# One decoder layer on one core: the self-attention regrouped into a score phase and a value phase

## The chip, the cores and the metric

The kernel runs on one core of one Trainium2 chip. The metric is device time in microseconds, the median of the runs shown; less is better. The core has a matrix engine (TensorE, in the profile PE, its weight loads PEld), VectorE (DVE), ScalarE (ACT), GpSimd (POOL) and SyncE (SP), and 16 DMA engines that move data between on-chip memory and HBM. In this kernel SP and POOL issue the DMAs. Matrix products go to eight PSUM banks of 128 x 512 float32 and are carried from there by ScalarE or VectorE.

## The reference

`x` is 4 batches of 512 rows of 512. Three blocks follow one another, each with a layer norm before it and a residual after it:

```python
x = x + attn(layernorm(x), Wq, bq, Wk, bk, Wv, bv, Wo, bo)   # 16 heads
x = x + xattn(layernorm(x), ctx, ctx, gamma)                 # 8 heads, cross attention
x = x + ffn(layernorm(x), w1, w3, w2)                        # ternary weights, silu gate

def attn(x, ...):                      # T=512 rows, 128 channels a head
    q = (x @ Wq + bq).reshape(B, T, 128, 16)   # and k, v
    q = transpose(q, (0, 3, 2, 1))             # channels x rows
    k = transpose(k, (0, 3, 1, 2))             # rows x channels
    v = transpose(v, (0, 3, 2, 1))             # channels x rows
    att = softmax(q @ k / sqrt(128))           # 128 x 128, a head
    return reshape(att @ v) @ Wo + bo
```

The attention is between channels, not between rows: a head's score matrix is 128 x 128, whatever the number of rows. The feed-forward's weights are quantized to -1, 0, 1 times a scale (the mean of the absolute values); its hidden width is 1365.

## The kernel before, in words

**What is multiplied.** Since scores are q'·k over the rows, the kernel never builds q and k. For each batch it takes the normalised rows X, forms the gram matrix G = X'X (512 x 512; `gram_upper`, L422, computes the blocks on and above the diagonal, `gram_rest`, L451, turns the others on TensorE), then y = G·Wk for a quarter of the heads (`keys_of`, L483; a quarter is four heads, 512 columns, index j) and the scores Wq'·y, four 128 x 128 blocks (`scores`, L503, with the softmax). On the other side u = X'·Wo-part (`values_out`, L468), m = Wv'·u (`values_of`, L493), and the result rows are the sum over heads of turned scores times m (`output`, L545, into four accumulators a batch that start as x plus the bias). `turned` (L540) transposes the scores on TensorE.

**Split products.** A plain float32 product is 16 matmuls, each done as two passes. A split product (`products`, L329) has its operands in three float32r parts, h, l and d (`Tri`, `tri_of`, L187: h on ScalarE, l and d on VectorE): per pair of output blocks 16 matmuls h and l into one bank each (L336, L337), a copy to memory by ScalarE (L343, a tile of `a_t`), 8 matmuls of d (L348), and one VectorE operation that joins them (`total`, L356). A split product is 48 matmuls.

**Batch 0** (L865 to L939) brings the raw weights of each quarter (`first_weights`, L234; the last row of a weight is folded in, L255, to take account of the bias row), makes their parts and keeps them in HBM for the other batches (`keep_weights`, L258, with DMAs issued by POOL; q is kept unsplit). While parts are being made, six of its twelve products are plain (`products_f32`, L363): u and y of quarter 0 and the m of all four quarters (`FIRST`, L213).

**Batches 1 to 3** (L977 to L1021) load the kept parts of o, k and v and the kept q (`weights`, L302, DMAs issued by SP into the 18 buffers of `a_w`; in batch 1 the missing d parts are made, L322, and kept) and run for every quarter u, y, m and the scores; turned scores and outputs come one quarter later. Beside them, in small steps taken at each `tick` of a product, run the quantization of the feed-forward's weights (`quantize`, 73 steps over three batches) and the cross attention of the batch before (`cross`, L680: scores in two matmuls, maximum and scaling on VectorE, exponential on ScalarE, transposes, and a product with 64 columns). The cross attention of batch 3 runs in the feed-forward.

**The feed-forward** (L1055 to L1130) loads the quantized weights as three resident tiles t1, t3 and t2 and runs h1, h3 (L1084) and y (L1119) for each batch.

**Order.** The code is written for a planner that orders each engine's instructions: it takes the earliest in the program that it reckons to be ready, so an instruction that is not ready is passed by later ones, and the order is then fixed for the run. Semaphores keep it right. `issue_after` and `gate_of` (L218: a constant that is computed from a given tile, so that what uses it can't be placed before that tile is there) hold work back. Each engine and each issuing queue goes through its list in order, and a waiting instruction holds what is behind it.

**Memory.** On-chip memory is a stack from the left and one from the right (`side="right"`), and it is nearly full. A pool that is closed makes room for later ones, whose tiles wait until the old tiles in that place are done with (`reuse_waits="tile"`: for each tile by itself).

## Time and profile before

| | |
|---|---|
| time, median of 3 runs | 1152.13 us (1150.59 to 1153.99) |
| span of the profiled execution | 1150.0 us |
| median of the runs less that span | 2.1 us |
| busy: TensorE, weight loads, VectorE, ScalarE, GpSimd | 99%, 75%, 71%, 46%, 26% of the span |
| granted TensorE clock | 0.999 |
| moved by DMA | 270.68 MB |
| batch 0 (first matmul of its gram to the next gram) | 6.90 to 190.25 us |
| next grams, of batches 1, 2, 3, start at | 190.25, 409.28, 624.51 us |
| first feed-forward matmul | 852.45 us |

The profile's page gives busy time by engine, a picture of the span in slices, the DMA queues, the chain of work that ended last, and the costliest groups of instructions. A time on its own, as "0.44 us", is a duration; "at 104 us" is counted from the span's start. A matmul is pipelined: its duration (some 0.39 us for 512 float32r columns) is longer than the distance to the next, so a busy share near 100% alone does not say how much time a set of matmuls takes. The distance between the starts of neighbours does.

### The profile page before, as it was taken

What the parts mean: (1) busy time and instruction counts of PE and PEld (TensorE: products, weight loads), DVE (VectorE), ACT (ScalarE), POOL (GpSimd) and SP (SyncE); (2) the same over time, 40 slices, a digit from 0 to 9 for tenths busy, and PEclk for the clock granted to TensorE, in tenths of its full rate; (3) what the DMA queues carried; (4) which work ended last, traced back from release to release, by engine and by line L of the source; (5) the groups of instructions that cost most, each with busy time, mean ns of one, the idle gap of its engine ahead of it and who ended that gap; (6) DMA issues with size and microseconds to landing.
All of it is one profiled execution on the core that took longest, in us unless ns stands there. A gap on an engine that the chain in (4) does not pass through costs nothing.

```text
span 1150.0 us, 16662 instructions
## 1 busy us (share of the span) xinstructions
PE 1140.7 (99%) x5310; PEld 858.6 (75%) x5310; DVE 818.7 (71%) x1818; ACT 523.5 (46%) x1071; POOL 295.9 (26%) x534
## 2 busy tenths in 40 slices
PE   9999999999999999999999999999999999999998
PEld 5486585787778767877776787777778877777886
DVE  6857766978788965969696769788857856536242
ACT  4534334354535442644354445445355768534020
POOL 3435433433133232213221422122113212000000
PEclk9999999999999999999999999999999999999999
DMA  9999996998889769988986798799791422122100
GB/s 332 306 344 337 345 314 225 324 319 280 281 281 308 261 201 325 312 272 276 321 291 215 256 334 271 254 330 325 268 304 40 122 79 65 48 73 72 64 1 37
DMA packets 146177, 270.68 MB, mean 235 GB/s; under 512 B 18276, under 2 KB 49300, under 8 KB 146090
## 3 DMA queue, kind: packets, MB, share of 16 engines
q1 hardware_dynamic: 112218, 164.93, 43.4%
q0 software_dynamic: 33872, 104.70, 26.8%
q8 instruction: 42, 0.69, 0.2%
q14 instruction: 45, 0.37, 0.1%
HBM read 206.62 MB, written 62.93 MB: 234 GB/s over the span
## 4 chain that ended last, share of the span: by engine, by line
PE 96%; DMA 2%; DVE 1%; issue 1%; ACT 0%; POOL 0%; SPq 0%; DVEq 0%; POOLq 0%; ACTq 0%
PE h L1084 13%; PE y L1119 7%; PE xo L770 5%; PE xp L126 5%; PE po L548 5%; PE pm L370 5%; PE sc L509 5%; PE pg L430 3%; PE xs L727 3%; PE xs L726 2%; PE pu_2h L336 1%; PE pu_1d L348 1%; PE py_3h L336 1%; PE py_3h L337 1%; PE pu_2h L337 1%; PE py_2h L337 1%
## 5 line engine op out<-in xcount | busy, mean ns | idle before, releaser
L1084 PE MATMUL h<-fxh,t 128*128 128x512 f32 (+1 forms) x352 | 139.6, 397 | 0.0
L1084 PE MATMUL h<-fxl,t 128*128 128x512 f32 (+1 forms) x352 | 137.4, 390 | 0.0
L737 ACT ACTIVATE p<-xs,xnmax 128x512 f32<-128x512 f32 x128 | 87.2, 689 | 84.8 <-PE xp L126 68.2
L731 DVE TENSOR_REDUCE xnmax<-xs 128x1 f32<-128x512 f32 x128 | 83.5, 684 | 19.3 <-PE xs L727 19.3
L1084 PEld LDWEIGHTS h<-fxh,t 128*128 128x128 f32 (+1 forms) x352 | 65.0, 185 | 15.4 <-issue 1.1
L1084 PEld LDWEIGHTS h<-fxl,t 128*128 128x128 f32 (+1 forms) x352 | 65.0, 185 | 14.7 <-issue 0.2
L1119 PE MATMUL y<-t,gh 128*128 128x512 f32 (+1 forms) x176 | 69.3, 394 | 0.0
L1119 PE MATMUL y<-t,gl 128*128 128x512 f32 (+1 forms) x176 | 68.8, 391 | 0.0
L129 ACT COPY pt<-xp 128x512 f32<-128x512 f32 x96 | 54.1, 595 | 31.0 <-PE xp L126 31.0
L126 PE MATMUL xp<-ident,p 128*128 128x128 f32 x512 | 66.5, 273 | 0.0
L126 PEld LDWEIGHTS xp<-ident,p 128*128 128x128 f32 x512 | 59.3, 140 | 9.4 <-issue 2.4
L770 PE MATMUL xo<-pt,vals 128*64 128x512 f32 x256 | 61.5, 599 | 0.0
L1097 DVE SCALAR_TENSOR_TENSOR gf<-h,scales_w,sl 128x512 f32<-128x512 f32 (+1 forms) x44 | 32.9, 747 | 39.8 <-PE h L1084 36.4
L749 DVE TENSOR_SCALAR p<-p,xrden 128x512 f32<-128x512 f32 x128 | 56.7, 486 | 2.9
L548 PE MATMUL po<-m,eT 128*128 128x512 f32 x128 | 57.6, 593 | 0.0
L1093 ACT ACTIVATE sl<-h,scales_w 128x512 f32<-128x512 f32 (+1 forms) x44 | 30.1, 688 | 58.7 <-PE h L1084 58.5
L689 POOL DMA_DIRECT2D xd<-x_a x64 | 33.8, 532 | 88.6 <-DVE qs L710 64.5
L370 PE MATMUL pm<-u,v_raw 128*128 128x512 f32 x128 | 55.6, 592 | 0.0
L727 PE MATMUL xs<-kl,qs 128*128 128x512 f32 x128 | 50.1, 391 | 0.5 <-DVE kl L714 0.5
L138 POOL CAST gh<-gf 128x512 fp32r<-128x512 f32 (+1 forms) x24 | 15.8, 660 | 134.9 <-DVE gf L1097 119.7
L726 PE MATMUL xs<-kh,qs 128*128 128x512 f32 x128 | 50.1, 392 | 0.0
L139 DVE TENSOR_TENSOR gl<-gf,gh 128x512 fp32r<-128x512 f32 (+1 forms) x44 | 30.4, 690 | 26.3 <-POOL gh L138 19.3
(313 smaller groups left out, 2897.6 us busy)
## 6 DMA issues: line engine op xcount, KB each, us to landing
oh<-kept_oh SPq DMA_DIRECT2D x48, 256.0 KB, 5.9
ol<-kept_ol SPq DMA_DIRECT2D x48, 256.0 KB, 6.2
kh<-kept_kh SPq DMA_DIRECT2D x48, 256.0 KB, 5.2
kl<-kept_kl SPq DMA_DIRECT2D x48, 256.0 KB, 5.9
vh<-kept_vh SPq DMA_DIRECT2D x48, 256.0 KB, 6.6
vl<-kept_vl SPq DMA_DIRECT2D x48, 256.0 KB, 6.9
q<-kept_q SPq DMA_DIRECT2D x48, 256.0 KB, 6.6
od<-kept_od SPq DMA_DIRECT2D x44, 256.0 KB, 6.8
```

Of the source, the lines that this page charges most:

```text
L126: nc.tensor.transpose(pt[:, ts(k, P)], src[:, ts(k, P)], ident)
L370: nc.tensor.matmul(p, lhsT=lhs(k)[:, ts(i, P)], rhs=rhs(k), start=(k == 0), stop=(k == 3))
L509: nc.tensor.matmul(sc[:, ts(g, DH)], lhsT=w[k][:, ts(g, DH)], rhs=ys[k][:, ts(g, DH)], start=(k == 0), stop=(k == KC - 1),)
L548: nc.tensor.matmul(po, lhsT=eT[:, g, :], rhs=ms[g], start=True, stop=True)
L726: nc.tensor.matmul(sc, lhsT=q[:, ts(m, P)], rhs=kh, start=True, stop=False)
L727: nc.tensor.matmul(sc, lhsT=q[:, ts(m, P)], rhs=kl, start=False, stop=True)
L731: nc.vector.reduce_max(nmax[:, i : i + 1], scs[i], axis=AX.X)
L737: nc.scalar.activation(p, scs[i], AF.Exp, bias=nmax[:, i : i + 1], scale=xscale, accum_out=den[:, i : i + 1],)
L749: nc.vector.tensor_scalar(ps[i], ps[i], rden[:, i : i + 1], None, ALU.mult)
L770: nc.tensor.matmul(po[half, :], lhsT=vals[c][:, l, half], rhs=pt[j][:, l, :], start=(l == 0), stop=(l == NC - 1),)
L1084: nc.tensor.matmul(ph[:r, :], lhsT=t[:, block(i, k)], rhs=fxT[j][:, k, :], start=(k == 0 and j == 0), stop=(k == KC - 1 and j == 1),)
L1119: nc.tensor.matmul(py, lhsT=g[i][j][:r, ts(c, P)], rhs=t2[:r, i, :], start=(i == 0 and j == 0), stop=(i == NHC - 1 and j == 1),)
```

## The change

The attention is regrouped into two phases.

**Score phase.** Sixteen steps, quarter by quarter and within each over the four batches. A step runs y (`keys_of`), then the scores of the step before, then turns the scores of two steps before. The k weights of a quarter are brought raw, folded and split once and stay on chip for its four steps (`keys_halves`, `keys_thirds`); q is folded once a quarter (`queries_folded`) after y of batch 1, by the newest gate. All four batches' split gram matrices stay on chip (those of batch 0 in the buffers of x's parts); rows are normalised and their grams formed ahead of, and during, the first steps. `y` tiles and gram matrices share eight buffers. Normalised rows go to HBM (`kept_x`), so do the turned scores (`kept_e`), written over the scores' own tile. From step 4 on, beside the products, the parts of o and v are made and kept (`kept_weights`, 32 pieces, DMAs in and out issued by POOL, five buffers for the parts).

**Value phase.** Batch by batch and quarter by quarter u, m and the output, with the rows and turned scores loaded back; all of these products are split. Weights come through 21 buffers. Quantization is spread over all four batches; cross attention of the batch before runs over the 48 ticks of a batch (42 in the last). Cross attention's second scaling moves from VectorE to ScalarE. The plain products and the parts they needed (`products_f32`, `FIRST`, `first_weights`, `keep_weights`) are gone.

The diff, cut to its core:

```diff
-    x3p, xnp, g3p, u3p = apool("a_x3", 12), apool("a_xn", 4), apool("a_g3", 1), apool("a_u3", 12)
-    yp, tp = apool("a_y", 5), apool("a_t", 3)
-    ep, mp, accp = apool("a_e", 1), apool("a_m", 4), apool("a_acc", 4)
+    x3p, tp, ep = apool("a_x3", 12), apool("a_t", 3), apool("a_e", 3)
...
+    def fold(k, t, last, gate):
+        less = gate[2 if k == KC - 1 else 1]
+        nc.vector.scalar_tensor_tensor(t, last, less, t, ALU.mult, ALU.add)
+
+    def halves_of_weight(h, l, t, gate):
+        nc.scalar.mul(h, t, gate[0])
+        nc.vector.scalar_tensor_tensor(l, h.bitcast(F32), -S, t, ALU.mult, ALU.add)
+
+    def third_of_weight(tri):
+        nc.vector.tensor_tensor(tri.d, tri.l.bitcast(F32), tri.h.bitcast(F32), ALU.subtract)
+
+    def keys_halves(j, k, raw, gate):
+        last, chunks = raw
+        fold(k, chunks[k], last, gate)
+        h, l = (kp.tile([P, GW], F32R, tag="k", name=f"k{p}_{j}_{k}") for p in "hl")
+        halves_of_weight(h, l, chunks[k], gate)
+        keys[j][k] = Tri(h, l, None)
...
+        coming = []
+        for item in itertools.chain(items(), [None]):
+            if item is not None:
+                coming.append((item[:3], bring(*item[:3])))
+                if len(coming) < 2:
+                    continue
+            (n, j, k), t = coming.pop(0)
+            gate = gates[0]
+            if n == "v":
+                fold(k, t, sources[j][0], gate)
+            tri = Tri(
+                *(pool.tile([P, GW], F32R, tag="made", bufs=5, name=f"{n}{p}_{j}_{k}") for p in "hld")
+            )
+            halves_of_weight(tri.h, tri.l, t, gate)
+            third_of_weight(tri)
+            for p, part in zip("hld", (tri.h, tri.l, tri.d)):
+                nc.gpsimd.dma_start(kept[n, j, p][ts(k, P), :], part.bitcast(F32))
+            yield
...
     def turned(b, j, e):
-        eT = ep.tile([P, NG, DH], F32, tag="eT", name=f"eT_{b}_{j}")
-        transpose_blocks(eT, e, f"pe_{b}_{j}", True)
-        return eT
+        transpose_blocks(e.rearrange("p (g t) -> p g t", g=NG), e, f"pe_{b}_{j}", True)
+        nc.gpsimd.dma_start(kept_e[b, j], e)
+
+    def turned_kept(b, j):
+        e = ep.tile([P, GW], F32, tag="e", name=f"eT_{b}_{j}")
+        nc.gpsimd.dma_start(e, kept_e[b, j])
+        return e
...
-            for i in range(2):
-                nc.vector.tensor_scalar(ps[i], ps[i], rden[:, i : i + 1], None, ALU.mult)
+            nc.vector.tensor_scalar(ps[0], ps[0], rden[:, 0:1], None, ALU.mult)
+            nc.scalar.mul(ps[1], ps[1], rden[:, 1:2])
...
+    kp, yp = apool("a_k", 20, phase_a), apool("a_y", 8, phase_a)
+    g3p = {b: apool(f"a_g3_{b}", 1, phase_a) for b in (3, 2, 1)}
+    qp = apool("a_q", 4, phase_a, side="right")
+    krp = apool("a_kr", 4, phase_a, side="right")
+    xpool = ExitStack()
+    xnp = apool("a_xn", 2 * NG, xpool, side="right")
...
+    grams[0] = gram_upper(0, xs)
+    raw_k = raw_all("k", 0, krp)
+    xs = rows_given(1)
+    for k in range(KC):
+        keys_halves(0, k, raw_k, gates[0])
+    normed(1, xs, False)
+    raw_q = raw_all("q", 0, qp)
+
+    def first_rest():
+        g3[0] = gram_rest(0, grams[0])
+
+    grams[1] = gram_upper(1, xs, first_rest)
+    keys_thirds(0)
...
+    for n, (j, b) in enumerate(STEPS):
+        if n == 4:
+            xpool.close()
+            ovp = apool("a_ov", 1, phase_a, side="right")
+            side = Side(kept_weights(ovp), KEPT_STEPS, 6 * (len(STEPS) - n) - 4)
+        if n < 2:
+            xs = rows_given(n + 2)
+            normed(n + 2, xs, False)
+        ys[n] = keys_of(b, j, g3[b], keys[j], side.tick)
+        gates[0] = gate_of(ys[n][3])
+        if n < 3:
+            g3[n + 1] = gram_rest(n + 1, grams[n + 1])
+        if n < 2:
+            grams[n + 2] = gram_upper(n + 2, xs)
+        if b == 1:
+            queries_folded(j)
+        if n > 0:
+            scored(n - 1)
+        if b == 0 and n > 0:
+            raw_q = raw_all("q", j, qp)
+        if b == 0 and j + 1 < HG:
+            raw_k = raw_all("k", j + 1, krp)
+        if b in (1, 2) and j + 1 < HG:
+            for k in CHUNKS[2 * (b - 1) : 2 * b]:
+                keys_halves(j + 1, k, raw_k, gates[0])
+        if b == B - 1 and j + 1 < HG:
+            keys_thirds(j + 1)
+        if n > 1:
+            turn(n - 2)
+        if n == len(STEPS) - 3:
+            xs = rows_kept(0, krp, "raw_k")
+        if n == len(STEPS) - 2:
             x3 = parts_of(0, xs)
...
+    side.rest()
+    scored(len(STEPS) - 1)
+    phase_a.close()
...
+    u3p, mp = apool("a_u3", 12), apool("a_m", 4)
+    accp, xnp, bop = apool("a_acc", 8), apool("a_xn_kept", 4), apool("a_bo", 1)
...
-        for n, k in (("a_w", 18), ("a_stage", 3))
+        for n, k in (("a_w", 21), ("a_stage", 3))
...
+    PRODUCT = 6
+    TICKS = 2 * HG * PRODUCT
+    quant = Side(quantize(), QUANTIZE_STEPS, B * TICKS - PRODUCT)
...
+    for b in range(B):
         for j in range(HG):
             u3 = values_out(b, j, x3, weights("o", b, j, wp), tick)
-            if j > 0:
-                waiting[2] = turned(*waiting[:3])
-            ys = keys_of(b, j, g3, weights("k", b, j, wp), tick)
-            if j > 0:
+            if b == 0 and j == 0:
+                turn(len(STEPS) - 2)
+                turn(len(STEPS) - 1)
+            if waiting:
                 output(*waiting)
...
+                if b > 0:
+                    side = Side(
+                        itertools.chain(row_norms(b - 1, accs), cross(b - 1, *cpool)),
+                        NORM_STEPS + CROSS_STEPS,
+                        TICKS if b + 1 < B else TICKS - PRODUCT,
+                    )
+                accs = accumulators(b)
...
+            eT = turned_kept(b, j)
             ms = values_of(b, j, weights("v", b, j, wp), u3, tick)
-            e = scores(b, j, weights("q", b, j, wp), ys)
...
+            waiting = [b, j, eT, ms, accs]
```

## The prediction

> **What bounds the kernel now.** I read the share of the span by engine, the chain, TensorE's own waits, then busy time by stretches. The first three lines are from the page, the waits follow.
>
> ```profile
> span 1150.0 us, 16662 instructions
> PE 1140.7 (99%) x5310; PEld 858.6 (75%) x5310; DVE 818.7 (71%) x1818; ACT 523.5 (46%) x1071; POOL 295.9 (26%) x534
> ...
> PE 96%; DMA 2%; DVE 1%; issue 1%; ACT 0%; POOL 0%; SPq 0%; DVEq 0%; POOLq 0%; ACTq 0%
> ```
>
> ```profile
> PE py_0d L348 <- DMA kd<-kept_kd: 1.0, 2, 0.6
> PE pm_0d L348 <- DVE vd L322: 0.9, 1, 0.9
> PE pu_1d L348 <- DMA od<-kept_od: 0.7, 1, 0.7
> ```
>
> TensorE runs from 6.90 us to the end with almost no holes, 96% of the chain is its work, and its waits on weights come to 2.6 us. So the change is worth what it takes off TensorE, less every new hole. Durations of single matmuls overlap; what counts is the spacing in the chain:
>
> ```profile
> 15.80 13.74 PE pu L370 x32
> ...
> 86.95 13.73 PE pm L370 x32
> ...
> 107.90 1.81 PE pu_2d L348 x8
> 113.34 1.81 PE pu_2d L348 x8
> 118.78 1.82 PE py_2d L348 x8
> ...
> 623.51 1.00 PE xo L770 x2
> 624.51 1.91 PE pg L430 x4
> 626.43 3.58 PE xo L770 x14
> ```
>
> A plain f32 product (32 passes at L370) takes 13.74 us. A split product repeats its half every 5.44 us (107.90, 113.34, 118.78), so it takes 10.88 us. The last three lines show that the planner reorders TensorE: the gram matrix of the next batch stands later in the program than the cross attention it interrupts.
>
> By stretches (columns: length, busy time of PE, PEld, DVE, ACT, POOL with counts, clock, DMA share, GB/s):
>
> ```profile
> 104.00:147.00 43.00, 43.00 (x176) 29.60 (x174) 30.96 (x65) 16.34 (x33) 20.61 (x39) 1.00 1.01 357
> 216.00:262.00 46.00, 44.43 (x216) 36.59 (x215) 39.67 (x94) 22.62 (x47) 14.34 (x26) 1.00 1.01 337
> 350.00:404.00 54.00, 54.00 (x280) 42.51 (x279) 50.04 (x125) 28.71 (x64) 12.79 (x22) 1.00 0.84 278
> 420.00:460.00 40.00, 38.96 (x183) 31.03 (x182) 28.11 (x65) 14.20 (x26) 12.77 (x23) 1.00 0.88 289
> 625.00:680.00 55.00, 55.00 (x250) 41.01 (x249) 34.73 (x81) 18.28 (x35) 17.04 (x31) 1.00 0.81 263
> ```
>
> VectorE at 93% (350:404) costs TensorE nothing. The DMA engines are full at 337 to 357 GB/s; the stretch at 337 lost 1.57 us, the one at 289 lost 1.04, the one at 263 nothing.
>
> **Part 1, TensorE's work.** Six products of batch 0 are plain today (u and y of quarter 0, the four of m); afterwards all 48 are split: 6 x (13.74 - 10.88) = 17.2 us less. All else on TensorE keeps its count: 4 grams, 16 scores (3.57 each), 16 turns, 16 outputs (3.43 each), cross attention, feed-forward. **-17.2.**
>
> By mean duration nothing would be gained (48 x 392 ns = 18.8 us against 32 x 592 ns = 18.9). The Trainium skill (Perfetto Trace Analysis, Identifying the Most-Contended Engine) rejects matmul busy time as a measure and takes the weight loads' share instead. That share is 75% here and would leave a quarter of the engine to absorb every new hole of the parts below, for 1132 us; the spacing above shows no such room, so the sum goes by spacing.
>
> **Part 2, waits that go.** The k loads and the making of vd and od in batch 1 disappear: **-2.6**, the three lines of waits.
>
> **Part 3, the start.** TensorE's first gram ends at 15.8 and was followed by a plain product on weights already there. Now the gram of batch 1 follows and needs that batch's rows normalised. On SP's queue they come behind the k weights: issue of x ends at 2.6, k_last takes 0.43, four k_raw 4.59, the rows 1.82, so the rows are issued from 7.6 to 9.4 and, at 4.7 us to landing, are there from 12.3 to 14.1. VectorE then needs the last statistics (0.68 + 0.17), the root (0.30, ScalarE), the reciprocal (0.15), the first tile (0.54 + 0.06): 16.0, a hole of 0.2. But four folds and four low halves of k (8 x 0.69 = 5.5 us) stand ahead of it; VectorE is free of batch 0 at 10.7, so 1.6 of them fit before 12.3 and 3.9 do not: hole 4.1. Ends: 0 (rows first) and 5.7 (none fits). **+4.1**, by program order.
>
> **Part 4, steps 0 to 3.** VectorE carries three row norms (about 7 us each), four gram splits (8 x 0.69 = 5.5 each), totals, scores and the next k: some 82 us by sum, against 85 of TensorE. Besides, the gram matrices and the y tiles share 8 buffers: y of step 1 and 2 wait until a gram is split, which stands behind them in the program, and TensorE goes on only as far as its 8 banks reach. Ends: 0 (20 to 60 us ran with VectorE at 28.10 of 40.00 and no hole) and 5.5, one gram split exposed. **+1**, near the first row.
>
> **Part 5, the other score steps.** One takes 10.88 + 3.57 + 0.44 = 14.9 us. In four steps (59.6 us) VectorE has 16 totals 10.9, four scores 8.7 (0.69, 0.17, 0.18, 4 x 0.284), q folds 3.0, k 8.5, gates 1.8, and 11.3 kept pieces of o and v at 1.75 each, 19.7: 52.6, or 88%, under the 93% that cost nothing. The q fold is gated on y of batch 1, so that step's scores are ready only two totals, a gate and four folds later (1.4 + 0.45 + 3.0 = 4.8). Behind them on TensorE stand a turn and the next product, which the planner can take first, as with pg above: 0; unfilled, in steps 5, 9 and 13, 14.4. The kept pieces use five buffers for three parts each: a part is held for making (0.72 + 2 x 0.69), an issue on POOL (0.54) and a landing (4.0 to 7.1 by the store rows), 6.6 to 9.7 us, so a piece can follow every 4.0 to 5.8 us; one is wanted every 5.6: 0, other end 32 x 0.2 = 8. POOL issues four DMAs a piece, 2.2 of 5.6 us, and SP loses the k and q loads: 0. **0.**
>
> **Part 6, values of batch 0.** 4 x (2 x 10.88 + 3.43) = 100.8 us, with no cross attention beside it. Transfers, in tiles of 0.262 MB: weights 96, quantization 22 (73 steps over 186 ticks, 48 here), turned scores 4, accumulators and bias 5, rows 4, result 4: 135, or 35.3 MB, 350 GB/s. The 21 weight buffers lie on the gram tiles of batches 1 and 2, free by the last score step, so 12 or more tiles come ahead: 32.2 MB, 319 GB/s. The nearest row is 337 GB/s, losing 1.57 in 46: 3.4 in 101. Ends: 0 (357) and 13.8 (nothing comes ahead, at the 308 GB/s of the first 20 us: 114.6 us for 35.3 MB). **+3.4.**
>
> The Trainium skill (DMA: Bandwidth & Descriptors, Where 436 GB/s comes from) puts the HBM limit of a core at about 358 GB/s, which would make this part 0 and the sum 1142; two full stretches here differ by 20 GB/s, so the slower one stays in the sum.
>
> **Part 7, first quarters of batches 1 to 3.** There cross attention is only starting: some 44 tiles, 11.5 MB, 34.2 us at 337, against about 27.5 on TensorE; nine spare buffers cover 7.0. Nearest rows are today's first quarters (1.57, 1.04, 0): **+2.6** in all. Ends 0 and 3 x 6.7 = 20. VectorE over such a batch: 140 us by sum; measured busy in 404 to 625 is 171.3 where the same count gives 185, so 130 of 145: 0. If the last quarters run out of VectorE, 3 each. The scaling moved to ScalarE takes 64 x 0.486 = 31 us from VectorE: 0, ScalarE is half idle.
>
> **Part 8, into the feed-forward.** Its second weight tile (t3) now lies on the turned scores and the u parts, in use until the last output; before it lay on x and gram tiles. Two h products (1.83 each) need only t1; the first piece of t3 (512 KB) takes 1.5 us by bytes at 337 and 8.0 by its row under load. **+2**; ends 0 and 6.2.
>
> **Sum.** 1150.0 - 17.2 - 2.6 + 4.1 + 1 + 0 + 3.4 + 2.6 + 2 = 1143.3. The median of the runs, 1152.13, stands 2.1 above the profiled span: **1145.4 us**.
>
> **Rivals.** *All hides*: every new hole at its lower end, 1150.0 - 19.8 + 2.1 = 1132. For it: TensorE is covered almost everywhere today, and less is moved in all. Against it: the start has nothing else to run.
>
> *The values phase starves* (slower): parts 6 and 7 at 13.8 + 20 in place of 6.0: 1173. For it: these stages lose score work that covered loads; the demand is 319 to 420 GB/s where today's first quarters wait at 289. Against it: 357 was reached. Less what comes ahead and what the spare buffers hold, 32.2 + 3 x 9.1 = 59.5 MB must pass in 100.8 + 3 x 27.5 = 183 us; the sum passes today's median at a loss of 12.7 us here, that is, below about 304 GB/s.
>
> *Scores wait in line* (slower): the gated folds uncovered, 14.4: 1160. Against it: the reordered pg; for it, that a queue's order is fixed before any landing is known.
>
> **How the numbers follow.** Chances: the sum's case 0.42, all hides 0.20, starving 0.20, scores in line 0.12, others slower 0.06. A change of 0.3% (3.5 us, to 1148.7 or 1155.6) is about what this kernel's runs can tell. The sum's case alone spans 1138 to 1153: two thirds of it faster, a quarter same. Faster 0.20 + 0.28 = 0.48; same 0.11; slower the rest, 0.41. The range goes from all hides, 1132, to the starving case, 1173.
>
> **What would show it.** Right: split products in batch 0 at 5.44 us a half; a hole of about 4 us after the first gram; DMA share near 1.0 in batch 0's values with a few us of TensorE waiting for vh or od. Wrong: longer waits on o and v tiles in each first quarter, scores that follow their product after 4 to 5 us of idle, VectorE waiting for landings of kept pieces, or a TensorE spacing other than 10.88 us.

## The result and the profile after

The changed kernel takes 1231.09 us (median of four runs, 1230.42 to 1232.23), against 1152.23 us for the kernel before beside it: 1.0684 times, interval 1.0669 to 1.0699. It is 79 us slower; the prediction was 1145.4, with a range up to 1173. The page of the profile after (span, busy time, slices, clock, chain):

```profile
span 1228.9 us, 16751 instructions
PE 1150.6 (94%) x5406; PEld 888.6 (72%) x5406; DVE 822.5 (67%) x1766; ACT 568.9 (46%) x1141; POOL 312.4 (25%) x556
...
PE   7999999999899877999969999898998999999998
...
PEclk9999999999899987999979999989998999999999
...
PE 26%; ACT 1%; DMA 1%; DVE 0%; issue 0%; ACTq 0%
```

TensorE is busy for 94% of the span, formerly 99%, with dips a third of the way in, at the half and at two thirds. The slices of the granted clock, nines throughout before, dip with them. The chain is followed back only some 28% of the span, through the feed-forward and the last cross attention, and so says nothing of the phases that matter here. The waits of TensorE do (waiting line and releaser: us, times, longest):

```profile
PE xs L716 <- DVE qs L700: 30.4, 3, 17.1
PE po L539 <- DVE u L359: 9.0, 2, 5.8
PE pg L414 <- DVE xn L383: 5.5, 2, 5.1
PE h L1058 <- DMA t<-t_w: 5.2, 1, 5.2
PE sc L496 <- issue: 5.1, 2, 2.7
PE pm_0h L337 <- ACT uh L191: 3.3, 2, 2.2
PE sc L496 <- ACT oh L257: 2.4, 1, 2.4
```

The longest line shown of before was 1.0 us in all. Now the first cross-attention scores of batches 1 to 3 of the values phase wait 17.1, 11.1 and 2.2 us for their operand. No o or v tile is in this list. By stretches (length, busy time of PE, PEld, DVE, ACT, POOL with counts, clock, DMA share, GB/s; values of batch 0, then three stretches with cross attention):

```profile
318.00:418.00 100.00, 97.47 (x395) 75.74 (x395) 67.63 (x143) 27.53 (x49) 17.68 (x30) 0.97 0.92 324
418.00:565.00 147.00, 126.51 (x548) 92.22 (x547) 112.77 (x242) 75.12 (x151) 42.79 (x77) 0.91 0.77 256
565.00:730.00 165.00, 149.63 (x675) 108.47 (x673) 125.51 (x274) 86.39 (x174) 53.24 (x92) 0.95 0.81 263
730.00:920.00 190.00, 176.40 (x829) 126.28 (x828) 144.17 (x325) 105.59 (x215) 46.89 (x85) 0.98 0.71 231
```

In the second and third no engine and no queue is full: TensorE 86 and 91%, VectorE 77 and 76%, the transfers under those of batch 0. That points to order, not to capacity: an engine stands at the head of its list for something that another has not done.

**Where the 79 us are.** Add up the distances between neighbouring matmul starts and take three parts: the spacing that a matmul of its kind has when nothing disturbs it, idle time between one's end and the next's start, and the rest, spacing stretched. The idle time is read from the trace; the other two are estimates, as they depend by a few us on what is taken as undisturbed.

| us | before | after | difference |
|---|---|---|---|
| undisturbed spacing | 1128.2 | 1111.2 | -17.0 |
| idle | 4.0 | 73.2 | +69.2 |
| stretched | 12.1 | 39.0 | +26.9 |

What is added to the stretched part lies in windows in which the granted clock is 0.5: ten of them after (75 us in all, some 27 us of stretch), none before until the last 3.9 us. They begin within a hole or up to 1.2 us after its end (at 21.6 us in the one that ends at 21.8, at 199.1 after one that ends at 198.5, at 455.1 in the 17-us hole) and last 3.4 us or a multiple. A window of 3.4 us costs some 1.7 us. So of 96 us lost 69 are holes, and some 27 the clock that goes with them.

The idle time by place: start 6.1; score steps 7.5; values of batch 0 4.3; from 420 us to the feed-forward 54.6 (30.4 of it the cross scores, 9.0 the outputs, 5.2 the feed-forward's weight tile, a hole from 925.2 to 930.3 us).

**The 17-us hole, line by line.** Timeline of TensorE (start, duration, what, in brackets the idle time before and its releaser), then of VectorE, then of POOL:

```profile
450.51 1.98 PE L349 MATMUL pu_1d<-od,xd 128*128 128x512 f32 x8
469.62 0.79 PE L716 MATMUL xs<-kh,qs 128*128 128x512 f32 x1 [17.14 <-DVE qs L700]
```

```profile
438.00 0.17 DVE L96 BATCH_NORM_AGGREGATE mv_c<-st_c 128x2 f32<-128x6 f32 x1
443.85 0.69 DVE L955 TENSOR_TENSOR acc<-acc,bo_bc 128x512 f32<-128x512 f32 x1 [5.67 <-DMA acc<-in_x_dram]
...
448.46 0.69 DVE L955 TENSOR_TENSOR acc<-acc,bo_bc 128x512 f32<-128x512 f32 x1 [2.50 <-DMA acc<-in_x_dram]
...
450.26 0.17 DVE L662 COPY mv_c<-rstd_c 128x4 f32<-128x4 f32 x1
...
457.62 0.16 DVE L586 TENSOR_TENSOR abs_w<-abs_w,one 128x1 f32<-128x1 f32 x1 [4.01 <-DMA abs_w<-in_w3t_dram]
...
466.69 0.16 DVE L586 TENSOR_TENSOR norms<-norms,one 128x1 f32<-128x1 f32 x1 [5.45 <-DMA norms<-norm_a]
...
468.81 0.75 DVE L700 SCALAR_TENSOR_TENSOR qs<-xd,norms,qs 64x512 fp32r<-64x512 f32 x1
```

```profile
451.19 0.54 POOL L574 DMA_DIRECT2D abs_w<-in_w3t_dram  x1 [4.93 <-DMA t_w<-tern_w]
453.12 0.54 POOL L574 DMA_DIRECT2D abs_w<-in_w3t_dram  x1 [1.40 <-DMA t_w<-tern_w]
453.65 0.55 POOL L663 DMA_DIRECT2D norm_a<-mv_c  x1
...
460.07 1.40 POOL L666 DMA_DIRECT2D norms<-norm_a  x2 [4.60 <-DMA norm_a<-mv_c]
```

The row statistics of batch 0 are complete at 438.2. Joining them ends at 450.4, because VectorE's list has additions of the output bias ahead, which wait for landings. The store of the statistics leaves at 453.7, behind POOL's wait for a buffer of the quantization. It lands, is read back at 460.1, and VectorE, after 4.0 us for another landing, has them at 466.7. This way to HBM and back is called the trip below. From 452.5 us on the next scores are first in TensorE's list.

### The profile page after: what moved, and what is told of

It reads as the page before. It is cut to its first block, busy times and chain, and to the rows that moved or that the text cites. A ratio compares the mean times of both kernels' runs of the same rounds, so it can differ in the third digit from the quotient of the medians.

```text
span 1228.9 us, 16751 instructions
## 1 busy us (share of the span) xinstructions
PE 1150.6 (94%) x5406; PEld 888.6 (72%) x5406; DVE 822.5 (67%) x1766; ACT 568.9 (46%) x1141; POOL 312.4 (25%) x556
## 5 line engine op out<-in xcount | busy, mean ns | idle before, releaser
L1058 PEld LDWEIGHTS h<-fxh,t 128*128 128x128 f32 (+1 forms) x352 | 66.1, 188 | 21.6 <-issue 6.6
L716 PE MATMUL xs<-kh,qs 128*128 128x512 f32 x128 | 51.7, 405 | 30.8 <-DVE qs L700 30.4
L539 PE MATMUL po<-m,eT 128*128 128x512 f32 x128 | 64.6, 649 | 9.0 <-DVE u L359 9.0
L496 PE MATMUL sc<-y,q_raw 128*128 128x128 f32 x512 | 63.0, 280 | 7.5 <-issue 5.1
L496 PEld LDWEIGHTS sc<-y,q_raw 128*128 128x128 f32 x512 | 62.2, 196 | 10.7 <-issue 5.9
L191 ACT ACTIVATE uh<-u 128x512 fp32r<-128x512 f32 x64 | 40.3, 631 | 62.5 <-DVE u L359 62.2
L760 PE MATMUL xo<-pt,vals 128*64 128x512 f32 x256 | 58.5, 599 | 0.0
L539 PEld LDWEIGHTS po<-m,eT 128*128 128x128 f32 x128 | 25.7, 207 | 41.1 <-issue 23.4
```

The lines of the kernel that those rows point to most:

```text
L191: nc.scalar.mul(tri.h, src, H_OF)
L496: nc.tensor.matmul(sc[:, ts(g, DH)], lhsT=w[k][:, ts(g, DH)], rhs=ys[k][:, ts(g, DH)], start=(k == 0), stop=(k == KC - 1),)
L539: nc.tensor.matmul(po, lhsT=eT[:, ts(g, DH)], rhs=ms[g], start=True, stop=True)
L716: nc.tensor.matmul(sc, lhsT=q[:, ts(m, P)], rhs=kh, start=True, stop=False)
L760: nc.tensor.matmul(po[half, :], lhsT=vals[c][:, l, half], rhs=pt[j][:, l, :], start=(l == 0), stop=(l == NC - 1),)
L1058: nc.tensor.matmul(ph[:r, :], lhsT=t[:, block(i, k)], rhs=fxT[j][:, k, :], start=(k == 0 and j == 0), stop=(k == KC - 1 and j == 1),)
```

## The experiments

Each run is compared with runs of the kernel before on the same chip; these had medians from 1150.9 to 1152.5 us. "Idle" is the sum defined above, of which the change has 73.2 us, 54.6 of it between 420 and 931 us.

### Side work spread over fewer ticks, in the kernel before

The first expectations speak of three theories. A: the side steps come too thick for the ticks they have. B: the quantization's pieces, with their loads and stores, hold the lists of POOL and VectorE. C: the DMA engines are full.

```diff
@@ kernel before, the row norms and cross attention beside a batch
-            TICKS + 6,
+            48,
```

> The kernel before with one number changed: row norms and cross attention are spread over 48 ticks of a batch in place of 78, so as thick as in the regrouped kernel. Theory A: holes of 10 us or more a batch at the first cross scores, time 1175 or more. Theory B: quantization there comes at 0.34 steps a tick, with slack; under 5 us in all, time 1150 to 1160. Theory C: the same bytes; no change.

1178.96 us, 1.0239 (1.0208 to 1.027), 27 us slower than the kernel before. Idle goes from 4.0 to 23.2 us, and the clock falls to 0.5 at 228, 457, 682 and 873 us.

```profile
PE xs L726 <- DVE qs L710: 14.7, 3, 8.7
PE pe L126 <- DVE e L535: 3.6, 1, 3.6
```

One number gives the old kernel waits at the same place (the longest 8.7 us, 17.1 in the change), so they don't need the two phases: fewer ticks between the steps are enough. It is a third of the loss only.

### Twelve empty steps ahead of the cross attention

```diff
-  itertools.chain(row_norms(b - 1, accs), cross(b - 1, *cpool)),
-  NORM_STEPS + CROSS_STEPS,
+  itertools.chain(row_norms(b - 1, accs), [None] * 12, cross(b - 1, *cpool)),
+  NORM_STEPS + 12 + CROSS_STEPS,
```

> The regrouped kernel with 12 empty steps between the row norms and the cross attention of each batch (85 steps on a batch's ticks in place of 73). After the change TensorE is idle 30.4 us in three waits of the first cross scores (17.1, 11.1, 2.2), all behind the row norms' way through memory and back. Theory A (steps come too thick: 73 on 48 ticks, formerly on 78): the scores come some 5 ticks (about 11 us) later; the waits fall from 30.4 to under 8, time about 1231 - 25 = 1206. Theory B (quantization's staged pieces hold the queues of GpSimd and VectorE): the delay covers part of it, waits 5 to 15, time 1205 to 1220, and holes of the later kind stay. Theory C (DMA engines full, as the slower rival of the prediction had it): no change over 5 us.

1221.56 us, 1.0609 (1.0577 to 1.0641). The waits of the cross scores on qs go from 30.4 to 1.3 us, yet only 9.5 us are won: idle is 60.2, and the largest wait is now

```profile
PE po L539 <- DVE u L359: 12.3, 2, 8.3
```

with 4.5 us of cross scores on ScalarE's exponentials and 4.1 of outputs behind them. So the slack (the name of these empty steps below) is taken from the steps behind it.

### The quantization left out

```diff
-        for piece, t, i in ahead(pieces, f"abs_{name}"):
...
+        nc.vector.memset(scales[name], 1.0)
...
-        for piece, t, i in ahead(pieces, f"tern_{name}"):
...
+        for src, places in pieces:
+            for columns, place in places:
+                part = src[:, columns]
```

The sums, thresholds and signs are gone, and the pieces are copied from HBM to HBM.

> The regrouped kernel with the quantization left out: no sums, no thresholds, scales set to one; the feed-forward's weights are copied from memory to memory in the places of its later steps, so that no staged piece stands in the queues of VectorE and GpSimd. (The feed-forward's result is not the reference's.) Theory B: the first cross scores wait under 5 us in all in place of 30.4, the holes of 5.9 and 3.1 us before outputs go too; time about 1231 - 45 = 1186 or less. Theory A: the ticks are as dense as before, so at least 15 us of the 30.4 stay, time 1200 to 1215. Theory C: 18 MB of 252 fall away, 7%: some 10 us, 1220.

1204.69 us, 1.0463 (1.0432 to 1.0493): 26 us less, the largest gain of a single edit that leaves TensorE's products in place. Idle between 420 and 931 us falls from 54.6 to 25.7. The cross scores still wait 8.3 and 5.3 us, between what theories A and B gave; the start is worse (10.7 us of waits of the first grams, 6.1 with the quantization).

### The score steps: gate, rows and kept pieces

Two runs. In the first the q fold is gated by the second y tile in place of the fourth, and batch 1's rows are loaded and normalised ahead of the k weights:

```diff
-            queries_folded(j)
+            queries_folded(j, gate_of(ys[n][1]))
...
-    raw_k = raw_all("k", 0, krp)
     xs = rows_given(1)
-    for k in range(KC):
-        keys_halves(0, k, raw_k, gates[0])
+    raw_k = raw_all("k", 0, krp)
     normed(1, xs, False)
+    for k in range(KC):
+        keys_halves(0, k, raw_k, gates[0])
```

> The regrouped kernel with two places of the score phase moved, far apart in time: the q fold is gated on the second y tile of its step in place of the fourth, and the rows of batch 1 are loaded and normalised ahead of the first k split. The three holes at the scores (2.4, 2.4, 2.7 us, two of them followed by 3.4 us at half clock) should go, as no work stands between the product and its scores in the fixed order: -7.5 and -3.7. The 5.1 us hole in the second gram should fall to about 1 if the order of VectorE's work makes it, with 1.7 of half clock: -5.5; if the rows' landing makes it, it stays at 3 or more. Sum: 1231 - 17 = 1214, or 1219 without the second part. The waits at the cross scores stay at 30 (theories A to C alike).

1226.47 us, 1.0652 (1.0621 to 1.0683). The hole at the start goes from 5.1 to 1.7 us and takes its half clock with it. The holes ahead of the scores don't go but grow, to 3.5, 4.3 and 3.1 us. VectorE's list ahead of the first of them:

```profile
126.90 1.28 DVE L359 SCALAR_TENSOR_TENSOR y<-py_1t,py_1d 128x512 f32<-128x512 f32 x2
...
130.03 1.28 DVE L359 SCALAR_TENSOR_TENSOR y<-py_1t,py_1d 128x512 f32<-128x512 f32 x2
131.34 0.34 DVE L221 TENSOR_SCALAR gate<-y 128x1 f32<-128x1 f32 x4
...
132.41 2.73 DVE L254 SCALAR_TENSOR_TENSOR q_raw<-q_last,gate,q_raw 128x512 f32<-128x512 f32 x4
```

The first two y tiles are done at 128.2, but both gates (two operations each) are computed only behind the fourth tile, at 131.3: the edit didn't bring the folds forward, and put a gate more ahead of them. VectorE also waits there for the landing of a kept piece (3.4 us). The second run takes that wait away: the third part of a kept piece isn't made, so that five buffers serve two parts each.

```diff
-            third_of_weight(tri)
-            for p, part in zip("hld", (tri.h, tri.l, tri.d)):
+            for p, part in zip("hld", (tri.h, tri.l, tri.l)):
```

> The moved gate and rows (as in the run before) and, besides, only two parts made of each kept piece of o and v: the third is left out and the second is stored twice in its stead, so the value phase computes with a wrong third part. Five buffers now serve 2.5 pieces, not 1.7. With the gate moved alone the holes before the scores were 3.5, 4.3 and 3.1 us: VectorE stood 3.35 us waiting for the landing of a kept part, ahead of the y totals that the gate needs. Theory D (the landings of the kept parts hold VectorE and with it the scores): VectorE's and ScalarE's waits on these landings vanish and the three holes fall from 10.9 to under 2 us in all, time 1226 - 11 - 3 to 5 of half clock = 1211. Theory E (it is the gate's own chain, two totals, a gate and the folds): holes stay at 2 to 3 us each, 1222 to 1226.

1224.65 us, 1.064 (1.0601 to 1.0679). VectorE waits 5.1 us on kept pieces, formerly 18.0, and none of it ahead of these scores; the holes are 3.1, 3.1 and 3.1 us:

```profile
PE sc L495 <- issue: 6.2, 2, 3.1
...
PE sc L495 <- ACT vh L257: 3.1, 1, 3.1
```

So the buffers aren't the cause; what is left is the chain of the gate itself (totals, gate, folds). No run shows what folds ahead of the last totals would give: here too the gates stand behind them, at 130.4, though VectorE was idle for 4.2 us before the last totals.

### Deeper loads, and deeper loads with slack

Six staging buffers and three loads of the quantization under way (of 21 weight buffers 18 stay):

```diff
-        for n, k in (("a_w", 21), ("a_stage", 3))
+        for n, k in (("a_w", 18), ("a_stage", 6))
...
+            if i >= 3:
+                here = coming.pop(0)
```

> The regrouped kernel with six staging buffers for the quantization in place of three and its pieces loaded three ahead in place of one; the weights' buffers go from 21 to 18 to make room. Theory B (a staged piece waits for a store to land, and holds GpSimd's queue and VectorE's): VectorE's waits on tern_w and abs_w vanish, the row norms' trip is not held up, and the holes in the value phase fall by half or more: the waits of the first cross scores from 30 to under 15, time about 1231 - 25 = 1206 (without any quantization it was 1205). Theory A alone (thick steps): under 8 us gained. Theory C (transfers short): fewer weight buffers make it slower, with new waits on oh and vh.

1223.09 us, 1.0626 (1.0596 to 1.0657). The cross scores wait 17.8 us instead of 30.4; in its place a product of u waits 7.7 us on VectorE's total of m, and VectorE's waits for accumulators grow from 16.7 to 24.3 us. Together with batch 1's rows first and the twelve empty steps:

> Deep staging, 12 empty steps before cross attention, and the rows of batch 1 first, together. If A and B are both right and add: first cross scores wait under 3 us, other holes of the value phase under 20, start 1.7; time 1231 - 5 (start) - 45 = about 1181. If they are two names of the same delay, no better than the better of the two alone (1206) less 5: 1201. Either way it does not reach 1152: the score phase's holes and the u splits before m remain.

1214.04 us, 1.0548 (1.0514 to 1.0582), idle 59.6, slower than both figures expected. Only 0.3 us of waits on qs is left, but 8.3 of u on m, 7.7 and 6.6 of cross scores on m and on exponentials.

### Two tries at the accumulators

Loads of a batch's accumulators asked for one batch earlier in the program, alone; with the statistics' trip issued by SP; and, without that, with rows, slack and deeper loads:

```diff
-                accs = accumulators(b)
+                accs = next_accs
+            if j == 1 and b + 1 < B:
+                next_accs = accumulators(b + 1)
...
-        nc.gpsimd.dma_start(norm_a[b].rearrange(
+        nc.sync.dma_start(norm_a[b].rearrange(            # second run only
```

> The regrouped kernel with the accumulators of a batch loaded in the second quarter of the batch before (those of batch 0 ahead of the value phase) in place of the first quarter of their own. Before the change a whole quarter lay between these loads and the bias added to them on VectorE, and VectorE never waited; now one product lies between, and VectorE stands 16.7 us in six waits for them, with the row norms, the y and u totals and the cross splits behind it in its list. Theory F (a load brought too near to its use, in a list that is worked in order): these waits go, the row norms' store is issued 5 to 8 us earlier in batches 1 and 2, and the first cross scores wait some 8 to 12 us less than 30.4: 1231 - 12 = 1219. Theory A or B alone: VectorE's wait moves on to the norms or the staged pieces, and TensorE gains under 4 us.

1228.15 us, 1.0664 (1.0633 to 1.0695).

> As the run before, and the row norms' way through memory (one store, two loads of 4 KB a batch) is issued by SP in place of GpSimd. Theory B (GpSimd's list, held by staged pieces, makes the trip late): the trip from reciprocal to landed norms was 20.8, 18.4 and 13.3 us in batches 1 to 3; it falls to about 13 (two landings of 4.5 to 7 us), the first cross scores' waits to under 12. If SP's own waits for weight buffers hold it as long, no gain over the run before.

1224.29 us, 1.0631 (1.06 to 1.0661). The trip, from VectorE's reciprocal of the root to the statistics' landing, shortens to 13.7, 13.8 and 9 us (20.8, 18.4 and 13.3 in the change), the waits on qs to 16.0 us, for 4 us of time.

> Rows of batch 1 first, deep staging, 12 empty steps before cross attention (together 1214) and the accumulators a batch ahead. Theory F: VectorE's 24 us of waiting on accumulators in the run without this goes, and with it the holes of 8.3 and 7.7 us in which TensorE waited for m totals: 1214 - 18 = 1196. If these totals were late for another reason, 1210 or more.

1213.56 us, 1.0537 (1.043 to 1.0645). Its two executions lie 10 us apart, so no gain or loss against 1214.04 can be told.

The first edit did not do what it says: in the run with it alone the last load is issued at 605.3 us, in the change at 608.2. Eight buffers hold two batches, so a batch's loads go when the stores of the batch two before have freed them, wherever the program asks. Later we moved the additions instead, one product later in the program:

```diff
             if waiting:
+                if waiting[1] == 0:
+                    biased(waiting[4])
                 output(*waiting)
...
-            if j == 0:
-                biased(accs)
```

> The change with one thing moved: the output bias is added to a batch's accumulators one product later, just ahead of the first addition into them, in place of right after the first product of m. VectorE waited 16.7 us for the landings of these loads in the change, and 32.4 us with the cross attention left out. If that wait, early in a batch, is what holds the statistics, the m and u pieces behind it (9.4 us of it stand between the root and the store of the row norms in batch 1), the wait of the first cross scores falls from 17.1 to about 8 us, that of po on u from 9.0 to about 3, and the time to 1210 to 1220 us. If the landings of the quantization's and the norms' loads simply take its place in the fixed order, it stays at 1226 to 1234.

1226.72 us, 1.0647 (1.0628 to 1.0666). Again the additions didn't move: they stand at 443.8 us as before, and VectorE waits 17.3 us for them. Where the 4 us of time come from is open.

### The cross attention left out

```diff
-  itertools.chain(row_norms(b - 1, accs), cross(b - 1, *cpool)),
-  NORM_STEPS + CROSS_STEPS,
+  copied_rows(b - 1),        # x_a to x_c, chunk by chunk, HBM to HBM
+  NC,
```

> The change with the row norms and the cross attention of batches 0 to 2 left out of the values phase: the rows they would have replaced are copied instead, one chunk to a step (the result is not the reference's; the last batch's cross attention and the feed-forward run as before). TensorE loses some 44 us in each of three batches (145 less the 101 of the value products), 132 in all. Side work too dense, with round trips on queues in fixed order: the waits of the cross scores on qs and of po on u between 420 and 925 us go with it, the holes of that stretch fall from about 45 us to under 10, and the time to 1231 - 132 - 50 = about 1045 us, 1035 to 1060. Transfers (the prediction's rival): the four batches of values now follow each other at about 100 us each and ask for some 350 GB/s without a pause, so TensorE waits on oh, od, vh and vd tiles, 10 us or more in each batch, and the time is 1065 to 1095 us.

1068.84 us, 0.9274 times the kernel before (0.9259 to 0.929): within the range expected of starving transfers, but not for its reason. TensorE's waits:

```profile
PE po L539 <- DVE u L359: 9.2, 2, 6.4
PE pu_1d L349 <- DVE m L359: 5.9, 2, 5.3
...
PE pm_2h L337 <- ACT uh L191: 4.6, 2, 4.1
PE pm_0h L337 <- ACT uh L191: 3.7, 2, 2.6
```

Not one matmul of the values phase waits on a weight tile, though the transfers run at 305 to 348 GB/s: the prediction's rival of starving transfers is refuted. Yet some 28 us of holes remain between 420 and 765 us without any cross attention, so its density isn't the whole cause either. VectorE's longest wait on a landing in this run is:

```profile
DVE acc L955 <- DMA acc<-in_x_dram: 32.4, 9, 10.4
```

### No quantization, slack, and the trip on SP

The edits of the second and third experiment, batch 1's rows ahead of the k weights, and the DMAs of the statistics on SP.

> Three edits at once: the quantization left out and its weights copied (the feed-forward's result is not the reference's), twelve empty steps between the row norms and the cross attention, and the trip of the row statistics issued by SP in place of POOL. If the waits on landings in VectorE's and POOL's fixed order are what the cross scores pay for, the edits add: the copied weights alone gave 1204.7, its waits of xs were 13.6 us with about 6 of half clock behind them, so about 1187 us, 1180 to 1195. If the empty steps only push the same work into a shorter stretch, as the other holes of the late cross attention suggest, new holes take their place and the time is 1198 to 1210 us. Neither theory lets it come below the kernel before: the holes of the start, the scores, the first values and the feed-forward, some 25 us with about 10 of half clock, stay in it.

1181.19 us, 1.0257 (1.0241 to 1.0272); idle 25.1, of which 10.7 between 420 and 931 us. The longest waits are those outside of the values phase:

```profile
PE sc L496 <- issue: 5.9, 2, 3.2
PE h L1034 <- DMA t<-t_w: 3.6, 1, 3.6
PE pg L414 <- DVE xn L383: 2.8, 1, 2.8
PE sc L496 <- ACT oh L257: 2.4, 1, 2.4
```

The same with the quantization back (and the bias later in the program), first without and then with the deeper loads:

> As the kernel with all edits but without the deeper staging (three buffers, one load under way, 21 weight buffers). If VectorE's waits on the landing of the quantization's pieces still cost, it is 8 us or more slower than the kernel with all edits (the deeper staging alone was worth 8.0 us); if the three weight buffers that the staging takes are worth as much, the two agree within 3 us.

> Nothing left out, every edit that puts distance between a load and its use: the late bias, the rows of batch 1 ahead of the k weights, twelve empty steps ahead of the cross attention, the trip of the row statistics on SP, and six staging buffers with three loads under way. If distance is what was missing, it comes near the run in which the quantization was left out: 1185 to 1200 us. If VectorE's and POOL's plain amount of work in a batch of 145 us is what binds, the deeper loads change little and it is 1205 to 1215, as the earlier run with rows, staging and empty steps.

1214.06 us, 1.0539 (1.052 to 1.0559), and 1210.73 us, 1.0509 (1.0492 to 1.0527). The two lie 3.3 us apart, so the landings of the quantization's pieces are a small part at this point. Put side by side, the two causes roughly add up: the single gains come to 43 us and 48 of idle, the joint one is 50 and 44.

| | idle 420 to 931 us | time |
|---|---|---|
| the change | 54.6 | 1231.1 |
| with slack, trip on SP, rows first, late bias | 35.1 | 1214.1 |
| without quantization | 25.7 | 1204.7 |
| both (without the late bias) | 10.7 | 1181.2 |

### The bias additions held in their batch

Sixteen loads and sixteen additions, four a batch in order: those at 443.8 to 451.7 us belong to batch 2, whose first output is added at 642.6, and those at 608.3 to 618.5 to batch 3, first output at 802.5. The group of the change (count: duration, first and last start) and what its idle time ended on:

```profile
L955 DVE TENSOR_TENSOR acc<-acc,bo_bc x16: 682/689/693, 310.2 to 618.5; 128x512 f32<-128x512 f32 x16
...
  DMA acc<-in_x_dram: 16.7, 6
```

They run 190 us before anyone needs them, and wait there for landings, ahead of the row statistics on which TensorE waits. The code's `issue_after` names a ScalarE copy; these start times show that it doesn't hold an addition on VectorE. Here the hold is data that VectorE itself computes:

```diff
-        with tc.issue_after(mark["copied"]):
-            for acc in accs:
-                nc.vector.tensor_tensor(acc, acc, bo_bc, ALU.add)
+        one = one_of(recent[-1])
+        for acc in accs:
+            nc.vector.scalar_tensor_tensor(acc, acc, one, bo_bc, ALU.mult, ALU.add)
```

> The change with the bias additions held in their own batch: each is multiplied by a one that VectorE computes from the newest copied product of that batch. In the change they run a whole batch early: those of batch 2 at 443.8 to 451.7 us for a first output at 642.6, those of batch 3 at 608.3 to 618.5 for one at 802.5, and VectorE waits there for the loads' landings (16.7 us in 6 waits), just where the row statistics of the batch before are to be joined. If this is what makes the first cross scores late, VectorE's waits on accumulators go, the 17.1 and 11.1 us of the cross scores fall by some 9 and 7, the holes around 315 us by a part, and the time is 1208 to 1220 us. If the landings of the quantization's pieces, in the same list, take the time back, it is 1225 to 1232, as with the bias moved in the program alone.

1220.0 us, 1.0596 (1.0573 to 1.0619): 11 us less for one edit that adds four short operations. The additions now stand in their batches and no landing of an accumulator is waited for:

```profile
L955 DVE SCALAR_TENSOR_TENSOR acc<-acc,one,bo_bc x16: 745/748/752, 325.7 to 772.3; 128x512 f32<-128x512 f32 x16
```

The 11.1 us of batch 2's cross scores become 5.3; the 17.1 of batch 1 only 16.2. There the next landings take over, and not on VectorE alone: the statistics are joined at 436.3 us, 14 earlier than in the change, but POOL issues their store only at 448.8, behind its own wait of 5.8 us for a store of the quantization to land. VectorE then waits 11.9 us for a piece of the quantization, and 18.3 us in four waits for the statistics.

> The bias held in its own batch, the rows of batch 1 ahead of the k weights, twelve empty steps ahead of the cross attention, and the statistics' trip on SP; nothing is left out. The same without the hold took 1214.1 us with 14.8 us of VectorE's waits on accumulators and 54 us of TensorE's holes. If early bias additions cost in this form too, 1198 to 1208 us; if the quantization's work on VectorE is what remains, within 4 us of 1214.

1208.12 us, 1.0478 (1.0462 to 1.0493), 6 less than without the hold.

> The kernel of the run before in this call with the quantization's six staging buffers and three loads under way added; nothing is left out. The same without the hold took 1210.7 us. All waits on landings that the trace showed in VectorE's list are then taken away, so what is left above the run without quantization (1181.2 us) is the quantization's work itself: 1190 to 1200 us if landings were most of it, 1205 to 1212 if the work is.

1197.31 us, 1.0395 (1.0364 to 1.0425), 13 less than without the hold, and the best with all work done. Here the deeper loads are worth 10.8 us, against 3.3 without the hold: with the additions out of the way the quantization's landings were VectorE's next waits (34 us in the run without them, 6 with). TensorE's longest waits:

```profile
PE xs L718 <- DVE qs L702: 7.5, 1, 7.5
PE sc L496 <- issue: 5.1, 2, 2.7
PE h L1060 <- DMA t<-t_w: 4.6, 1, 4.6
...
PE pu_1d L349 <- DMA od<-kept_od: 3.3, 1, 3.3
```

Rows first, slack, trip and deeper loads had won 20 us without the hold (1210.7); added to the hold they win 23. Together these edits, which leave all the work in place, are worth 34 of the 79 us. 16 us remain over the run without quantization, which had no hold. Some of that is the three weight buffers given up (od and vd are late by 5.6 us); how much is the quantization's own work on VectorE is open. No version that does all the work comes near the kernel before: the best has 48 us of idle time left, 32 of it between 420 and 931 us, and the cause of each of these holes was not tested one by one.

## Why the prediction was wrong

**Part 1, TensorE's work: right.** -17.2 predicted, -17.0 by the sum of spacings. The split product repeats its half in 5.44 us also in batch 0:

```profile
335.24 1.98 PE L349 MATMUL pu_1d<-od,xd 128*128 128x512 f32 x8
...
340.68 1.98 PE L349 MATMUL pu_1d<-od,xd 128*128 128x512 f32 x8
```

**Part 2: right.** The three lines of waits are gone.

**Part 3, the start: right but small.** 4.1 predicted, with 5.7 as the end for no fold fitting in; the hole is 5.1, with 0.6 and 0.4 beside it, and a half-clock window of some 1.7. Putting the rows first took 3.4 us of the hole away. That edit moved the rows' loads as well as the folds, so it doesn't tell them apart; but in the change VectorE works from 10.3 to 17.6 us without a pause, 5.5 us of it on the folds and low halves of k, which fits the folds.

**Part 4: right.** 1 predicted, none found between 25 and 130 us.

**Part 5, the score steps: sized at the wrong end.** 0 taken, 14.4 as other end; three holes of 2.4, 2.4 and 2.7 and two half-clock windows, some 11 us. The rival had the place and the mechanism. What failed is the argument by analogy: the planner did let the gram pass the cross attention in the old kernel, and was therefore expected to fill here too. The turn and the next product do come in, but behind the first score, when the hole is over. (The other end for the kept pieces, 32 x 0.2, is 6.4 and not 8; the sum doesn't use it.)

**Part 6, values of batch 0: right size, wrong reason.** 3.4 predicted for transfers; 4.3 of holes (with some 3 of half clock), none on a weight: the splits of u on ScalarE and VectorE come late for m. Transfers of 324 GB/s sufficed.

**Part 7, first quarters of batches 1 to 3: the step that failed.** It was sized by bytes against buffers, 2.6 us with 20 as upper end, and VectorE by its sum of work, "130 of 145: 0". Between 420 us and the feed-forward there are 54.6 us of holes (5.2 of them Part 8's) and some 16 of half clock behind them. VectorE's work was not underrated, it is 77% busy where 90% was forecast; what such a sum can't see is latency. In the old kernel the side steps of a batch were spread over 78 ticks in some 218 us; now over 48 in some 150, and the trips of the row statistics to HBM and back did not shrink with them: engines sat idle 12.5 and 8.0 us for the two landings (four batches) in the trace of before, 17.2 and 20.7 us after. The prediction treated cross attention as work to be hidden and left out the distance between a step and its user. Two further steps of the program were not costed: bias additions that run a batch early and stop VectorE's list (holding them is worth 11 us alone, 13 with the other edits), and the landings of the quantization, which stands in the prediction only in bytes and sums of work (leaving out all of it, work and landings, is worth 26 us alone). The early additions go with eight accumulator buffers in place of four: in the kernel before they begin 23 to 31 us ahead of the first output, here 194 to 199 in batches 2 and 3. How the holes divide among these causes is shown only as far as the edits go: of the 54.6 us, 32 are still there in the best run with all work, and 10.7 in the run with slack and without quantization.

**Part 8: near its upper end.** 2 predicted, end 6.2; the hole is 5.2, with 2.9 of half clock around it.

**The rivals.** "Starves" had the right place and sign and the wrong cause; its 1173 also set a range that could not hold 1231. "All hides" is refuted by every part from 3 on but the fourth; the weight loads' share, which spoke for it, is 72% after, and the holes were not absorbed. The list of what would make the prediction wrong named late scores and VectorE waiting on landings, but not landings beside the kept pieces.

**What no part had:** a hole costs more than its length. Sixty-nine us of holes brought some 27 us of half clock. The trace of before, with no hole over 0.9 us, couldn't show it. The Trainium skill (TensorE: Matmul & The Clock Gate, HAM oscillation — how this bites in real kernels) does give a rule, that idle gaps above about 3.4 us bring the halved clock back. It would have warned of the large holes. This case's trace goes further: a hole of 2.39 us at 196.1 was followed by a half-clock window at 199.1, one of 2.23 at 425.3 by a window at 427.8, and four holes of 0.4 to 1.2 us go with the window at 318.6, while one of 3.13 us at 846.0 was followed by none. So length alone doesn't decide and 3.4 is no safe limit.

## What to carry to other kernels

When work that runs beside the bound engine is pressed into a shorter stretch, price its round trips in time against the ticks that are left between a step and its user, not only its sum of busy time and bytes. In lists of fixed order an early instruction whose data is not needed for long can still stop everything behind it: look in the group's start times for work that stands a stage ahead of its user, and hold it by data on its own engine. Add to each expected hole of a few us its price in clock.

## What was unexpected of the hardware

The granted TensorE clock went to 0.5 in windows of 3.4 us or multiples of it, in or just behind holes, most of them of 2.2 us and more, and held the engine at half pace when its operands were there again: ten windows in the change, some 27 us of stretch for 69 us of holes. Also, an addition that was placed long before its use cost the bound engine 11 us: by the waits in the trace alone it would have been charged to the transfers.
